# Summing part of the second attention's weights on GpSimd in the first and the last batch element

## The chip, the cores and the metric

The kernel runs on one core of a Trainium2 chip. The metric is the device time in microseconds (us). The kernel before was run 7 times: median 3838.09 us, lowest 3835.74, highest 3838.99.

A core has five engines that run their own instruction streams in order and wait for each other through semaphores: TensorE (PE in the profile; its weight loads are listed as PEld), VectorE (DVE), ScalarE (ACT), GpSimd (POOL) and SyncE (SP, which here only issues DMAs).

## The reference, cut to what matters

The input holds 16 batch elements of 256 channels x 1024 positions, all in f32. Each element passes an attention of 4 heads of 64 (called a), a group norm, an attention of 8 heads of 32 (called b), a second group norm, and a two-layer network of 1024 hidden channels. Only attention b is touched by the change:

```python
attn = jnp.einsum('bhnd,bhmd->bhnm', q, k) * scale + phys_bias
attn = jax.nn.softmax(attn, axis=-1)
out = jnp.einsum('bhnm,bhmd->bhnd', attn, v)
```

The softmax divides each exponential by the sum of the exponentials over all 1024 keys. The kernel takes no maximum out first; it computes the exponentials e, multiplies them by v unnormalised, sums them up over the keys beside that, and divides at the end.

## The kernel before, in words

`first_pass` goes through the elements b = 0 to 15. Work of neighbouring elements is interleaved by hand: while `attention_b` of element b runs, `run` puts pieces of other work ("fill") between its steps: first the rest of its own query, key and value products, then the output products of the network of element b-1 and the query, key and value products of element b+1. Element 0 has no element before it, and its fill is only its own products. The last element has its own products and four pieces of the network of element 14; the other four of those pieces come after the attention. So in both of these elements some steps of `attention_b` stand bare, with nothing put between them.

`attention_b` (line 398 on) works through four items. An item is one block of 512 queries for one group of 4 heads (128 channels). An item is done in four units, at kb = 0, 2, 4 and 6; a unit covers two blocks of 128 keys. For each unit:

- `scores` (L422) makes 16 matmuls on PE, into all eight banks of PSUM: for the first key block two single banks (b0, b1) and one tile of two banks, for the second key block two tiles of two banks. ACT turns them into four SBUF tiles e of 128x1024 with five exponentials (L437). A matmul in f32 shows as two records in the trace, two passes.
- `add(..., 0)` adds the first two e tiles (first key block, head pairs 0 and 1) to the item's two sums `es` on DVE (L452). At kb = 0 there is nothing to add to yet, and `add(..., 1)` makes the sums from two pairs of tiles.
- `weigh` (L461) of the unit before runs on PE: 8 matmuls of e with v into bank b0. Its result is copied to `res` by ACT for kb = 0 (L475) and added to it by DVE for the others (L477). Only then can the next unit's scores use b0.
- `add(..., 1)` adds the other two e tiles to the sums, and is held in program order on DVE (`keep_in_program_order` puts an instruction behind the last one written for its engine).

The e tiles have 8 buffers, so a tile is written over two units later, after PE and the adding engine have read it.

When an item's last `weigh` has been issued, `normalise` follows one step later, that is at the end of the next item's first unit: 4 matmuls `den` (L485), one per head, against the ones-like weights `eones`, into bank b1. They add the sums over the 128 partitions; each writes 32 of the 128 PSUM partitions. `den_copy` (L282) copies the bank out on ACT, and the next unit's scores need b1 again. `denominators` then sends the rows to a compact tile by DMA on SP's queue, takes the reciprocal on DVE (L267), keeps two running checks on GpSimd (`dsum`, `isum`, L269 and L270), sends the reciprocals out and back in by DMA, and `scale` multiplies `res` by them on DVE (L500). After the second head group, `project` follows (`j`, PE).

The order on each engine is what a scheduler makes of the written order: an instruction goes early where its inputs are free, and the pinned ones stay.

## Time and profile before

The profiled execution took 3838.63 us, with a span of 3836.9 us from the first to the last instruction on the core; 1.7 us lie around it.

| | busy us | share of the span |
|---|---|---|
| PE | 3782.7 | 99% |
| PEld | 1509.3 | 39% |
| DVE | 2213.9 | 58% |
| ACT | 2033.8 | 53% |
| POOL | 84.7 | 2% |

The TensorE clock was granted at 0.999 of full speed. A busy share is a mean over stages of different kinds, and the end of a matmul is modelled, so PE at 99% doesn't mean that PE sets the pace everywhere. Where a group's line ends with "idle before, releaser", it tells how long the engine stood still before these instructions and what ended that. In a timeline, a row gives the start of a run of equal instructions, its length, engine, line, operation, tiles and, in brackets, the idle time just before it and what ended it. Times in it are counted from the start of the span.

### The profile page before, as it was taken

Reading aid. Unit: us, or ns where it says so; the run is one execution under the profiler, and the core shown is the slowest. Engines: PE = TensorE matmul, PEld = TensorE weight load, DVE = VectorE, ACT = ScalarE, POOL = GpSimd, SP = SyncE. Lnnn points to the kernel's source line nnn. Section 1 sums busy time; section 2 is a strip of 40 time slices with the busy share of each in tenths; the row PEclk is TensorE's granted clock in tenths of the full one; section 3 lists DMA queues with packets and bytes.
Section 4 is the critical chain, followed back from the end, with each engine's and each line's share of the span. In section 5 each row is a group of like instructions: output and inputs, shape, how many; then the busy total and the mean of one; then the engine's idle time right before and its main releaser. Section 6 shows DMA issues by size and latency. Waiting matters only on the chain.

```text
span 3836.9 us, 87391 instructions
## 1 busy us (share of the span) xinstructions
PE 3782.7 (99%) x38637; PEld 1509.3 (39%) x38637; DVE 2213.9 (58%) x2761; ACT 2033.8 (53%) x2625; POOL 84.7 (2%) x252
## 2 busy tenths in 40 slices
PE   8999999999999999999999999999999999999999
PEld 3334343333433334333343333433333333333435
DVE  4574646646466464665656556565564655646572
ACT  4555546555465554645546455454555545555461
POOL 1000000000000000000000000000000000000000
PEclk9999999999999999999999999999999999999999
DMA  2000000000000000000000001000000100000000
GB/s 83 10 16 12 30 12 16 27 12 30 12 16 27 12 30 12 19 29 7 30 12 22 26 10 32 7 33 15 13 30 7 32 15 13 29 7 25 12 13 23
DMA packets 62450, 78.58 MB, mean 20 GB/s; under 512 B 35344, under 2 KB 36880, under 8 KB 62064
## 3 DMA queue, kind: packets, MB, share of 16 engines
q1 hardware_dynamic: 57728, 68.72, 5.9%
q8 instruction: 304, 4.98, 0.5%
q10 hardware_dynamic: 3712, 3.80, 0.3%
q14 instruction: 82, 0.67, 0.1%
q0 software_dynamic: 624, 0.41, 0.0%
HBM read 54.54 MB, written 17.56 MB: 19 GB/s over the span
## 4 chain that ended last, share of the span: by engine, by line
PE 90%; DVE 5%; issue 2%; ACT 2%; DMA 0%; POOL 0%; ACTq 0%; SPq 0%; POOLq 0%; DVEq 0%
PE s_b L422 12%; PE m L709 12%; PE acc_b L461 12%; PE m L246 11%; PE s_a L303 10%; PE acc_a L324 9%; PE qk_b L246 6%; PE qk_a L246 6%; PE v_b L246 3%; PE j L246 3%; PE v_a L246 3%; DVE es_a L336 2%; PE o L246 2%; PE den_b L485 1%; ACT e_a L311 1%
## 5 line engine op out<-in xcount | busy, mean ns | idle before, releaser
L437 ACT ACTIVATE e_b<-s_b 128x1024 f32<-128x1024 f32 (+1 forms) x1280 | 982.7, 864 | 469.3 <-PE s_b L422 469.3
L452 DVE TENSOR_TENSOR es_b<-es_b,e_b 128x1024 f32<-128x1024 f32 x768 | 900.0, 1220 | 361.2 <-ACT e_b L437 361.2
L311 ACT ACTIVATE e_a<-s_a 128x1024 f32<-128x1024 f32 x512 | 521.4, 1025 | 450.1 <-PE s_a L303 438.2
L303 PE MATMUL s_a<-q,k 64*64 64x512 f32 x4096 | 562.2, 593 | 2.3 <-DVE x L533 2.3
L324 PE MATMUL acc_a<-e_a,v 64*64 64x512 f32 x4096 | 555.2, 589 | 0.0
L422 PE MATMUL s_b<-q,k 32*64 32x512 f32 x8192 | 536.3, 601 | 5.8 <-DVE res_b L477 4.9
L336 DVE TENSOR_TENSOR es_a<-es_a,e_a 128x1024 f32<-128x1024 f32 x384 | 469.0, 1221 | 111.5 <-ACT e_a L311 106.7
L461 PE MATMUL acc_b<-e_b,v 128*32 128x512 f32 x4096 | 492.1, 598 | 0.0
L709 PE MATMUL m<-gn_h,w 128*128 128x512 f32 x1024 | 459.9, 601 | 6.0 <-DVE mean_g L569 3.8
L246 PE MATMUL m<-g,w 128*32 128x256 f32 (+1 forms) x7616 | 464.0, 379 | 0.0
L246 PEld LDWEIGHTS m<-g,w 128*32 128x32 f32 (+1 forms) x7616 | 277.7, 112 | 215.8 <-issue 41.5
L717 ACT ACTIVATE g<-m,m1b 128x512 f32<-128x512 f32 x256 | 174.3, 687 | 341.9 <-PE m L709 341.7
L422 PEld LDWEIGHTS s_b<-q,k 32*64 32x64 f32 x8192 | 173.8, 130 | 293.9 <-issue 155.7
L324 PEld LDWEIGHTS acc_a<-e_a,v 64*64 64x64 f32 x4096 | 183.5, 133 | 260.6 <-issue 224.6
L709 PEld LDWEIGHTS m<-gn_h,w 128*128 128x128 f32 x1024 | 189.0, 190 | 244.4 <-issue 227.3
L303 PEld LDWEIGHTS s_a<-q,k 64*64 64x64 f32 x4096 | 167.5, 133 | 280.3 <-issue 199.1
L461 PEld LDWEIGHTS acc_b<-e_b,v 128*32 128x32 f32 x4096 | 108.5, 109 | 351.6 <-ACT e_b L437 194.7
L246 PE MATMUL qk_a<-x,wp 128*32 128x512 f32 (+1 forms) x1856 | 234.5, 594 | 9.4 <-DMA wp<-in_L_conv_w_proj_dram 6.5
L477 DVE TENSOR_TENSOR res_b<-res_b,acc_b 128x512 f32<-128x512 f32 x192 | 131.0, 682 | 190.9 <-PE acc_b L461 190.9
L246 PE MATMUL qk_b<-gn_g,wq 128*32 128x512 f32 (+1 forms) x1280 | 234.1, 592 | 0.0
L452 DVE TENSOR_TENSOR es_b<-e_b,e_b 128x1024 f32<-128x1024 f32 x128 | 150.7, 1219 | 52.4 <-ACT e_b L437 52.4
L639 DVE TENSOR_TENSOR v<-v_b,eones 128x512 f32<-128x512 f32 x64 | 43.8, 685 | 227.8 <-PE v_b L246 227.8
(112 smaller groups left out, 2068.7 us busy)
## 6 DMA issues: line engine op xcount, KB each, us to landing
x<-in_x_dram SPq DMA_DIRECT2D x32, 512.0 KB
rd_a<-row_a SPq DMA_DIRECT2D x64, 256.0 KB
rd_b<-row_b SPq DMA_DIRECT2D x256, 64.0 KB
out_dram<-x SPq DMA_DIRECT2D x64, 256.0 KB
w<-in_L_conv_mlp_w_dram ACTq DMA_DIRECT2D x2, 1024.0 KB
sp_b<-d_b SPq DMA_DIRECT2D x64, 8.0 KB
row_b<-inv_b SPq DMA_DIRECT2D x64, 8.0 KB
wq<-in_L_conv_qkv_w_dram ACTq DMA_DIRECT2D x1, 768.0 KB
```

Of the source, the lines that this page charges most:

```text
L246: nc.tensor.matmul(o[sl], w[:, sl], r, **flags)
L303: nc.tensor.matmul(s[h : h + HALF, g, :], kT[g * D : (g + 1) * D, c, kb * P + h : kb * P + h + HALF], qT[g * D : (g + 1) * D, c, t * TB : ...
L311: nc.scalar.activation(e, s, AF.Exp, scale=float(D) ** -0.5)
L324: nc.tensor.matmul(accs[i][h][g * D : (g + 1) * D, :], v[h * HALF : (h + 1) * HALF, kb, c * 2 + g], e[h * HALF : (h + 1) * HALF, g, :], st ...
L336: nc.vector.tensor_add(sums[i], held[i] if kb == 1 else sums[i], e)
L422: nc.tensor.matmul(outs[g][h : h + HALF, :], kT[g * D : (g + 1) * D, c, k0 : k0 + HALF], qT[g * D : (g + 1) * D, c, t * TB : (t + 1) * TB] ...
L437: nc.scalar.activation(to, s, AF.Exp, scale=float(D) ** -0.5)
L452: ins = nc.vector.tensor_add(d, es[n] if kb == 0 else d, es[2 * block + n])
L461: nc.tensor.matmul(acc[g * D : (g + 1) * D, :], v[:, kb + m, c * G + g], es[2 * m + g // 2][:, g % 2, :], start=(m == 0), stop=(m == 1),)
L477: nc.vector.tensor_add(r, r, acc)
L709: nc.tensor.matmul(ps, k["w1"][:, cc, hc * P : (hc + 1) * P], hn[0][:, cc, t * TB : (t + 1) * TB], start=(cc == 0), stop=(cc == CC - 1),)
L717: nc.scalar.activation(g, ps, AF.Gelu, bias=k["m1b"][:, hc : hc + 1])
```

## The change

In elements 0 and 15 alone, and only for units with kb = 2, 4 and 6, one of the two additions of `add(..., 1)`, that of head pair 1, is taken off DVE. GpSimd sums these tiles instead, into two tiles of 128x512 of their own (`apart`): it copies the two halves at kb = 2 and adds the two halves at kb = 4 and at kb = 6. In element 0 the tiles come from the buffers of the hidden layer (tag "g", 16 buffers); in element 15 they lie in a tile over the query buffer of attention a, which is free by then. `normalise` then has, for the heads of pair 1, two matmuls per head in place of one: the second adds the apart sums to the same PSUM rows.

```diff
+        helped, apart = b in (0, B - 1), {}
+        if b == B - 1:
+            spare = act.tile([P, CC, S], F32, tag="q0", name=f"spare_{key}")
...
             for n in range(G // 2):
                 d = sums[i][n]
+                if helped and block and n and kb:
+                    if kb == 2:
+                        apart[i] = [
+                            spare[:, i % 2, j * TB : (j + 1) * TB] if b else
+                            work.tile(
+                                [P, TB], F32, tag="g", name=f"ges_{key}_{i}_{j}", bufs=16
+                            )
+                            for j in range(2)
+                        ]
+                    for j, a in enumerate(apart[i]):
+                        e = es[2 * block + n][:, j, :]
+                        if kb == 2:
+                            nc.gpsimd.tensor_copy(a, e)
+                        else:
+                            nc.gpsimd.tensor_add(a, a, e)
+                    continue
                 ins = nc.vector.tensor_add(d, es[n] if kb == 0 else d, es[2 * block + n])
...
             for g in range(G):
-                nc.tensor.matmul(
-                    den[g * D : (g + 1) * D, :],
-                    k["eones"][:, c * G + g],
-                    sums[i][g // 2][:, g % 2, :],
-                    start=True,
-                    stop=True,
-                )
+                parts = [sums[i][g // 2][:, g % 2, :]]
+                if helped and g // 2:
+                    parts.append(apart[i][g % 2])
+                for m, part in enumerate(parts):
+                    nc.tensor.matmul(
+                        den[g * D : (g + 1) * D, :],
+                        k["eones"][:, c * G + g],
+                        part,
+                        start=(m == 0),
+                        stop=(m == len(parts) - 1),
+                    )
```

## The prediction

> **What bounds the kernel now.** I read the page's engine shares and its chain first, then windows over the two elements that change, then a timeline of one item in the bare stretch, then the POOL rows. On the page, PE leads with 99% and the chain that ended last is PE's:

> ```profile
> PE 90%; DVE 5%; issue 2%; ACT 2%; DMA 0%; POOL 0%; ACTq 0%; SPq 0%; POOLq 0%; DVEq 0%
> ```

> In elements 1 to 14 nothing is changed, so only the stage matters. Windows (length, then busy time of PE, PEld, DVE, ACT, POOL) show attention b of element 0 from its second item on, and the last element with fill and bare:

> ```profile
> 163.54:185.01 21.47, 19.94 (x204) 5.07 (x201) 18.74 (x20) 16.40 (x23) 1.28 (x2) 1.00 0.06 14
> 185.01:206.49 21.48, 19.95 (x205) 5.08 (x201) 18.75 (x20) 16.41 (x23) 1.29 (x2) 1.00 0.05 15
> ...
> 3683.41:3710.10 26.69, 26.69 (x396) 11.04 (x393) 18.44 (x22) 15.50 (x21) 0.22 (x1) 1.00 0.10 32
> ```

> A bare item takes 21.5 us and DVE is busy for 18.7 of them: near full, not full. With fill (last row) PE has no gap at all. So I went through a bare item row by row, in the timeline:

> ```profile
> 170.50 3.83 ACT L437 ACTIVATE e_b<-s_b 128x512 f32<-128x512 f32 x5 [1.17 <-PE s_b L422]
> ...
> 171.62 2.36 DVE L452 TENSOR_TENSOR es_b<-es_b,e_b 128x1024 f32<-128x1024 f32 x2 [0.66 <-ACT e_b L437]
> ...
> 173.90 0.68 DVE L477 TENSOR_TENSOR res_b<-res_b,acc_b 128x512 f32<-128x512 f32 x1
> 174.50 2.35 DVE L452 TENSOR_TENSOR es_b<-es_b,e_b 128x1024 f32<-128x1024 f32 x2
> ...
> 174.64 1.97 PE L422 MATMUL s_b<-q,k 32*64 32x512 f32 x30 [0.43 <-DVE res_b L477]
> ...
> 176.77 0.69 DVE L500 TENSOR_TENSOR res_b<-res_b,rd_b 128x512 f32<-128x512 f32 x1
> 177.37 2.35 DVE L452 TENSOR_TENSOR es_b<-es_b,e_b 128x1024 f32<-128x1024 f32 x2
> ...
> 179.64 0.68 DVE L477 TENSOR_TENSOR res_b<-res_b,acc_b 128x512 f32<-128x512 f32 x1
> 180.38 1.97 PE L422 MATMUL s_b<-q,k 32*64 32x512 f32 x30 [0.92 <-DVE res_b L477]
> ...
> 184.02 1.04 PE L485 MATMUL den_b<-es_b,eones 128*32 128x512 f32 x8
> 185.18 0.63 ACT L282 COPY d_b<-den_b 128x512 f32<-128x512 f32 x1
> ```

> The unit starts (first of the scores) lie at 163.54, 169.38, 174.64, 180.38 and 185.01, so the four steps of an item are 5.84, 5.26, 5.74 and 4.63. What ends each: the first, ACT (exponentials, then the copy of `res`, for which PE waits). The second, a latency: scores, exponentials (start 170.50), the two block-0 adds from 171.62 on, `res`, scores; DVE stood idle 0.66 ahead of it, so fewer adds don't shorten it. The third is the same loop, but DVE comes late: it still has the block-1 adds (174.50) and the multiplication (176.77) in hand. The fourth is PE: scores, `acc`, `den`, and the copy of `den` on ACT, which the next scores on bank b1 need.

> **What the change removes.** 24 adds of 128x1024 (two elements, four items, three units), 24 x 1.22 = 29 us of DVE. On the path lies only the third step, and there only what it has above the loop of the second: 5.74 - 5.26 = 0.48. It stands bare at three places (174.64 to 180.38, 196.11 to 201.85, 3721.20 to 3726.94). With fill, PE sets the step; at the fourth item's end too (`j` at 221.23 and 3746.32 follow `acc` without a gap). The most to be gained is 3 x 0.48 = 1.4 us.

> **What it adds on PE.** Eight times, two more matmuls, four more records. Eight records now start within 1.0 us in two rounds of four, 0.43 apart (the four heads sit on different columns of the array, and run side by side). The extra ones sit on the columns of heads 2 and 3, so these two need four rounds: 2 x 0.43 = 0.86 more. That the two heads' chains run side by side I take from the scores at 169.38: after one of the 16 matmuls went ahead alone, the first round holds eight records where the written order has a repeat of a position at the eighth, so a later matmul on a free position starts early:

> ```profile
> 169.38 0.71 PE L422 MATMUL s_b<-q,k 32*64 32x512 f32 x8 [0.18 <-ACT res_b L475]
> ```

> [...]

> Is it hidden? With fill, and where attention a or the network follows (`den` at 226.38, 3678.99, 3751.47), PE is full: 0.86 each. In the bare stretch the first scores (b0) wait for `res` until 184.95 anyhow, but b1 waits for the copy of `den`, which starts 0.1 after `den` ends, and the second exponential waits for b1 (0.25 idle). So all but some 0.06 passes on: 0.8. The sum is 8 x 0.8 = 6.4 us.

> **What it adds on GpSimd.** 16 copies and 32 adds of 128x512, for which there is no row. A memset on POOL takes 0.127 us for 128x16 and 0.223 for 128x128: 0.86 ns an element. The add of `dsum`, 128x16, takes 0.22. Lower end for the big add: 0.22 + 496 x 0.86 ns = 0.65 us (one pass). Upper end: two reads and a write in three passes, 1.5 us. I take two passes, 1.07, since two inputs must be read; a copy is 0.13 + 0.43 = 0.55.

> [...]

> GpSimd has the time: 5.4 us of a 21.5 us item. What counts is whom it stops. POOL's `dsum` takes 0.22 as a rule, but where it meets an es add it waits for its end:

> ```profile
> 166.38 1.06 POOL L269 TENSOR_TENSOR dsum<-dsum,sp_b 128x16 f32<-128x16 f32 x1 [44.41 <-DMA sp_b<-d_b]
> ...
> 166.14 4.66 DVE L452 TENSOR_TENSOR es_b<-es_b,e_b 128x1024 f32<-128x1024 f32 x4 [0.39 <-ACT e_b L437]
> ```

> The first of these four adds ends at 167.36, `dsum` at 167.44, between the first and the second. It goes the other way too: where POOL began 0.03 us ahead, the es add took 1.27 instead of 1.22:

> ```profile
> 467.17 0.22 POOL L270 TENSOR_TENSOR isum<-isum,inv_b 128x16 f32<-128x16 f32 x1
> ...
> 467.20 1.27 DVE L336 TENSOR_TENSOR es_a<-e_a,e_a 128x1024 f32<-128x1024 f32 x1 [0.17 <-ACT e_a L311]
> ```

> So a POOL add and a DVE add from two SBUF tiles exclude each other, and take turns. A short POOL read costs DVE 0.05; a read of 1.07 would cost about 1.

> Now the third step. The exponentials of the unit end at 170.50 + 3.83 = 174.33, and POOL's two adds are ready some 0.14 later (the delay from DVE's reciprocal to `isum`), just as DVE starts its remaining block-1 add at 174.50. Taking turns: DVE add 1.15 (pitch), POOL 1.07, DVE multiplication 0.6, POOL 1.07, two block-0 adds 2.3. `res` then starts at 174.50 + 6.19 = 180.69 instead of 179.64: 1.05 late, though an add has gone. [...] I take +1.0, three times: 3.0 us.

> At kb = 2 the copies meet a DVE that has 0.66 to spare and one add less; with fill the step has about 2 us of slack between `res` and the next scores. Nothing. At the end of the fourth item POOL's last add comes late for `den`: 222.69 ready, after the block-0 add at 223.64, POOL to 224.71, DVE's add to 225.85, POOL to 226.9 against `den` at 226.38 now. About +0.5 in both elements (0 to 1.2): 1.0 us. The tiles are free two units later than POOL needs them, SP's queue gets no new DMA, and behind POOL's new adds stand only `dsum` and `isum`, which nobody but the end check waits for.

> **The sum.** 6.4 + 3.0 + 1.0 = +10.4 us on 3838.63 of the profiled execution, 3849.0. That execution lies 0.5 above the median of the runs; I say 3849.

> **Rivals.**
> - *POOL stops nobody* (not slower): long reads share with DVE instead of excluding it. Place: the third step at its three bare places. Price: 6.4 - 1.4 = +5.0, 3843.6, within 0.2%. It decides as soon as the blocked time per POOL add falls below about 0.55. For it: the trace shows exclusion only with reads of 16 elements. Against: eight of eight met adds end 0.08 after the DVE add.
> [...]
> [...]
> - *`den` hidden*: the extra rounds run beside the next scores on heads 0 and 1's columns and b1 isn't waited for. Only 4.0, or 3842.6; with POOL harmless as well, the full gain, 3837.2.

> **How the numbers follow.** The forecast has 0.42, long adds 0.20, POOL harmless 0.20, strict order 0.08, `den` hidden 0.04, both hidden 0.06. What a measurement of this kernel can tell from no change is about 0.2%, 7.7 us: above 3845.8 is slower, below 3830.4 faster. Slower: 0.20 + 0.08 and nearly nine tenths of the forecast, 0.64. Faster: no case reaches it; 0.03 for a scheduler that orders things differently. Same: the rest, 0.33. The range from 3840 to 3858 leaves out only the full gain and what is worse than the long adds.

> **What would show it.** After: `den_b` with 12 records in four rounds, about 1.7 us long; POOL rows of 128x512, and their length; es adds on DVE of over 2 us in the bare units, or none; the third step at about 6.7 us or at 5.26; the fourth at about 5.4. I am wrong if long POOL reads don't hold DVE, if a POOL add is far from 1.07, or if the scheduler changes DVE's order.

## The result and the profile after

The changed kernel took 3847.09 us (median of 15 runs, 3845.59 to 3849.21), the kernel before beside it 3837.12 us (median of 35). That is 10.0 us slower; the ratio is 1.0026, with a 95% interval of 1.0019 to 1.0033. The profiled execution took 3847.57 us, with a span of 3845.8 us, 8.9 us more than the span before.

The page hardly shows it. These are the chain's shares and two groups of the changed kernel (a group's columns: busy us, mean ns of one, idle us before it and what ended that):

```profile
PE 90%; DVE 5%; ACT 2%; issue 2%; DMA 0%; POOL 0%; SPq 0%; ACTq 0%; POOLq 0%; DVEq 0%
...
L475 DVE TENSOR_TENSOR es_b<-es_b,e_b 128x1024 f32<-128x1024 f32 x744 | 880.6, 1231 | 375.4 <-ACT e_b L437 375.4
...
L422 PE MATMUL s_b<-q,k 32*64 32x512 f32 x8192 | 537.3, 603 | 8.9 <-DVE res_b L500 8.0
```

The same two groups before:

```profile
L452 DVE TENSOR_TENSOR es_b<-es_b,e_b 128x1024 f32<-128x1024 f32 x768 | 900.0, 1220 | 361.2 <-ACT e_b L437 361.2
...
L422 PE MATMUL s_b<-q,k 32*64 32x512 f32 x8192 | 536.3, 601 | 5.8 <-DVE res_b L477 4.9
```

DVE has lost its 24 adds, and yet PE's scores stood idle for DVE's `res` for 8.0 us, where the kernel before has 4.9. The mean of DVE's remaining adds went up, from 1220 to 1231 ns. These two lines fit what was expected of GpSimd, that it stands in DVE's way.

The time by steps needs the unit starts (first of the scores) of the two elements. An item has four units; the steps of the 16 units, in us, with the last one counted to the next matmul group:

| | items 1, 2, 3, 4 before | after |
|---|---|---|
| element 0 | 6.76 7.20 7.20 5.54; 4.63 5.85 5.25 5.74; 4.63 5.85 5.25 5.74; 4.63 5.85 5.25 9.76 | 6.75 7.20 7.20 5.47; 5.50 5.77 5.25 6.76; 5.49 5.77 5.25 6.77; **7.00** 5.77 5.25 10.64 |
| sum | 95.15 | 101.86 |
| element 15 | 6.76 7.20 7.20 5.54; 8.07 7.21 7.21 7.63; 4.64 5.85 5.25 5.74; 4.63 5.85 5.25 9.76 | 6.76 7.20 7.20 5.47; 8.95 7.21 7.21 7.59; 5.50 5.77 5.25 6.78; 5.49 5.77 5.25 10.64 |
| sum | 103.79 | 108.04 |

The prediction's "fourth step" (scores, `acc`, `den`, copy of `den`) opens a row's item here, because `den` of an item lies in the first unit of the next: 4.63 before, 5.50 after. Its "third step" is the item's last number: 5.74 before, 6.77 after. Between the two elements, from the end of element 0 to the first scores of element 15, nothing moved: 3421.30 us before, 3421.28 after.

So element 0 costs 6.7 us more and element 15 4.25 more, 10.96 in all. It comes from four sources: `den` eight times 0.86 to 0.88, together 6.9; the bare third step three times 1.03, 3.1; one step of 7.00 where its two fellows take 5.49, 1.5; and small gains of 0.04 to 0.08 in eight steps, 0.6 less. The span grew by less than 10.96, because in this execution the program's first scores came 2.1 us earlier. That is no gain of the change: over the profiles of this study the first scores came at any time from 129.5 to 132.5 us. In the kernel before they came at 132.20, and the granted clock was 0.50 from 16.42 to 19.82; in the changed kernel they came at 130.09, with a clock of 1.00 from 5 to 25.

The second item of element 0 in the changed kernel, from its second unit on (timeline of all engines; rows of weight loads and of SP are left out):

```profile
172.50 0.68 DVE L500 TENSOR_TENSOR res_b<-res_b,acc_b 128x512 f32<-128x512 f32 x1
173.08 4.04 POOL L473 TENSOR_TENSOR ges_b<-ges_b,e_b 128x512 f32<-128x512 f32 x2 [3.26 <-ACT e_b L437]
173.10 1.22 DVE L475 TENSOR_TENSOR es_b<-es_b,e_b 128x1024 f32<-128x1024 f32 x1
173.24 1.97 PE L422 MATMUL s_b<-q,k 32*64 32x512 f32 x30 [0.43 <-DVE res_b L500]
...
174.56 1.43 DVE L527 TENSOR_TENSOR res_b<-res_b,rd_b 128x512 f32<-128x512 f32 x1 [0.24 <-DMA rd_b<-row_b]
...
175.13 1.92 PE L484 MATMUL acc_b<-e_b,v 128*32 128x512 f32 x16
175.91 3.44 DVE L475 TENSOR_TENSOR es_b<-es_b,e_b 128x1024 f32<-128x1024 f32 x2
...
176.99 1.07 PE L422 MATMUL s_b<-q,k 32*64 32x512 f32 x2
...
179.27 0.68 DVE L500 TENSOR_TENSOR res_b<-res_b,acc_b 128x512 f32<-128x512 f32 x1
...
180.00 1.97 PE L422 MATMUL s_b<-q,k 32*64 32x512 f32 x30 [1.94 <-DVE res_b L500]
...
183.64 1.06 PE L512 MATMUL den_b<-es_b,eones 128*32 128x512 f32 x8
...
184.51 1.05 PE L512 MATMUL den_b<-ges_b,eones 128*32 128x512 f32 x4
...
185.63 0.58 ACT L282 COPY d_b<-den_b 128x512 f32<-128x512 f32 x1 [0.67 <-PE den_b L512]
```

Two things are to be seen. PE's scores at 180.00 stand idle for 1.94 us instead of 0.92, because `res` starts at 179.27. And `den` has a second row at 184.51, so its copy starts 1.99 us after its first record instead of 1.16.

The turns show one by one in the third item, where the timelines of DVE and of POOL in narrow windows keep the instructions apart:

```profile
196.38 1.22 DVE L475 TENSOR_TENSOR es_b<-es_b,e_b 128x1024 f32<-128x1024 f32 x1
...
197.51 1.76 DVE L527 TENSOR_TENSOR res_b<-res_b,rd_b 128x512 f32<-128x512 f32 x1
...
199.20 2.30 DVE L475 TENSOR_TENSOR es_b<-es_b,e_b 128x1024 f32<-128x1024 f32 x1
...
201.42 1.21 DVE L475 TENSOR_TENSOR es_b<-es_b,e_b 128x1024 f32<-128x1024 f32 x1
...
202.56 0.67 DVE L500 TENSOR_TENSOR res_b<-res_b,acc_b 128x512 f32<-128x512 f32 x1
```

```profile
196.36 2.36 POOL L473 TENSOR_TENSOR ges_b<-ges_b,e_b 128x512 f32<-128x512 f32 x1 [3.26 <-ACT e_b L437]
...
198.69 1.73 POOL L473 TENSOR_TENSOR ges_b<-ges_b,e_b 128x512 f32<-128x512 f32 x1
```

Waiting for the other engine is not shown as idle time but as a longer instruction. POOL's first add is 2.36 long, of which it waits out DVE's add (to 197.60). DVE's multiplication is 1.76 instead of 0.68: held by 1.08. DVE's first block-0 add is 2.30 instead of 1.22: held by 1.08 again.

### The profile page after: what moved, and what is told of

Read it like the earlier page. It is cut to its first block, busy times and chain, and to the rows that moved or that the text cites. A ratio compares the mean times of both kernels' runs of the same rounds, so it can differ in the third digit from the quotient of the medians.

```text
span 3845.8 us, 87438 instructions
## 1 busy us (share of the span) xinstructions
PE 3790.2 (99%) x38669; PEld 1514.9 (39%) x38669; DVE 2200.2 (57%) x2737; ACT 2033.4 (53%) x2625; POOL 159.0 (4%) x300
## 4 chain that ended last, share of the span: by engine, by line
PE 90%; DVE 5%; ACT 2%; issue 2%; DMA 0%; POOL 0%; SPq 0%; ACTq 0%; POOLq 0%; DVEq 0%
PE s_b L422 12%; PE m L736 12%; PE acc_b L484 12%; PE m L246 11%; PE s_a L303 10%; PE acc_a L324 9%; PE qk_b L246 6%; PE qk_a L246 6%; PE v_b L246 3%; PE j L246 3%; PE v_a L246 3%; DVE es_a L336 2%; PE den_b L512 2%; PE o L246 2%; ACT e_b L437 1%
## 5 line engine op out<-in xcount | busy, mean ns | idle before, releaser
L437 ACT ACTIVATE e_b<-s_b 128x1024 f32<-128x1024 f32 (+1 forms) x1280 | 982.5, 865 | 473.5 <-PE s_b L422 473.5
L475 DVE TENSOR_TENSOR es_b<-es_b,e_b 128x1024 f32<-128x1024 f32 x744 | 880.6, 1231 | 375.4 <-ACT e_b L437 375.4
L311 ACT ACTIVATE e_a<-s_a 128x1024 f32<-128x1024 f32 x512 | 520.7, 1024 | 450.6 <-PE s_a L303 438.0
L422 PE MATMUL s_b<-q,k 32*64 32x512 f32 x8192 | 537.3, 603 | 8.9 <-DVE res_b L500 8.0
L336 DVE TENSOR_TENSOR es_a<-es_a,e_a 128x1024 f32<-128x1024 f32 x384 | 468.9, 1221 | 111.6 <-ACT e_a L311 106.4
L422 PEld LDWEIGHTS s_b<-q,k 32*64 32x64 f32 x8192 | 174.8, 130 | 296.2 <-issue 161.6
L500 DVE TENSOR_TENSOR res_b<-res_b,acc_b 128x512 f32<-128x512 f32 x192 | 131.1, 683 | 196.6 <-PE acc_b L484 196.6
L475 DVE TENSOR_TENSOR es_b<-e_b,e_b 128x1024 f32<-128x1024 f32 x128 | 150.8, 1219 | 52.4 <-ACT e_b L437 52.4
```

What stands on the lines that cost most here:

```text
L311: nc.scalar.activation(e, s, AF.Exp, scale=float(D) ** -0.5)
L336: nc.vector.tensor_add(sums[i], held[i] if kb == 1 else sums[i], e)
L422: nc.tensor.matmul(outs[g][h : h + HALF, :], kT[g * D : (g + 1) * D, c, k0 : k0 + HALF], qT[g * D : (g + 1) * D, c, t * TB : (t + 1) * TB] ...
L437: nc.scalar.activation(to, s, AF.Exp, scale=float(D) ** -0.5)
L475: ins = nc.vector.tensor_add(d, es[n] if kb == 0 else d, es[2 * block + n])
L500: nc.vector.tensor_add(r, r, acc)
```

## The experiments

All times are medians beside the kernel before on the same chip; where a ratio stands, 9 to 11 runs are behind it, otherwise one. "Body" is the change of the two elements' step sums against those of before, from the profile of the run.

### The two parts of the change, each alone

**Only the longer `den`.** On the changed kernel, DVE does all the adds again, and GpSimd only fills its tiles with zeros for the second matmuls to read:

```diff
-                    for j, a in enumerate(apart[i]):
-                        e = es[2 * block + n][:, j, :]
-                        if kb == 2:
-                            nc.gpsimd.tensor_copy(a, e)
-                        else:
-                            nc.gpsimd.tensor_add(a, a, e)
-                    continue
+                        for a in apart[i]:
+                            nc.gpsimd.memset(a, 0.0)
```

> All adds back on DVE; GpSimd only writes zeros once per item (kb = 2), and the two extra den matmuls per item read these zeros. Theory (eight longer den stages, and GpSimd's reads in the way of DVE at three places): the den part alone, 8 x 0.86 = 6.9 us above before; the steps of a bare item 5.8, 5.26, 5.74, 5.5 us; no gap on PE above 1 us. Rival (all of the loss comes from GpSimd holding DVE): no change against before. Rival (den hidden in the bare stretch, only the three full places pay): 2.6 us above before.

Measured: 3844.76 against 3837.40, +7.4, ratio 1.0019 (1.0010 to 1.0028). Body +3.23 in element 0 and +3.36 in element 15. Every step with `den` is 0.86 to 0.88 longer, the third step is still 5.74 and its gap 0.92:

```profile
181.00 1.97 PE L422 MATMUL s_b<-q,k 32*64 32x512 f32 x30 [0.92 <-DVE res_b L495]
...
184.64 1.06 PE L507 MATMUL den_b<-es_b,eones 128*32 128x512 f32 x8
185.51 1.05 PE L507 MATMUL den_b<-ges_b,eones 128*32 128x512 f32 x4
```

From the start of `den` to the end of its last record it is 1.92 us, 0.87 of it added. About seven of the ten microseconds are this.

**Only GpSimd's adds.** On the changed kernel, the second matmuls of `den` are dropped:

```diff
-                if helped and g // 2:
-                    parts.append(apart[i][g % 2])
```

> As the changed kernel, but den is left with its four matmuls, so the part that GpSimd sums is missing from the denominators. Theory: 3 x 1.02 = 3.1 us above before from the third step, less 0.2, and 1.5 more in an execution where the TensorE clock falls to half behind a gap; 3 to 4.5 us above before, third step 6.76, fourth step 4.63. Rival (den makes up all of the loss): at or 1.4 us below before.

Measured: 3843.52 against 3837.40, +6.1, ratio 1.0017 (1.0008 to 1.0026). That is more than expected. The steps tell why: the third step is 6.77, as in the changed kernel, so GpSimd's price is there, three times 1.03. But the step behind it is 4.64 once, and 6.29 and 6.31 the other two times in element 0. There the granted TensorE clock was halved. PE's rows at the first of these places:

```profile
179.06 3.60 PE L422 MATMUL s_b<-q,k 32*64 32x512 f32 x30 [1.95 <-DVE res_b L500]
...
184.35 1.03 PE L510 MATMUL den_b<-es_b,eones 128*32 128x512 f32 x8
```

Thirty score records take 3.60 us instead of 1.97. A window over this place (length; busy us of PE, PEld, DVE, ACT, POOL; granted clock; DMA share; GB/s) gives the clock:

```profile
179.00:183.00 4.00, 3.94 (x34) 1.06 (x38) 1.62 (x2) 2.08 (x4) 2.74 (x2) 0.57 0.01 2
```

So there is a third term that the prediction doesn't have: some 1.7 us on the step behind each halved clock. Without these two longer steps the body would be +2.7.

**GpSimd writes zeros, DVE keeps its relief.** On the changed kernel, the copies and adds become zero fills:

```diff
-                        if kb == 2:
-                            nc.gpsimd.tensor_copy(a, e)
-                        else:
-                            nc.gpsimd.tensor_add(a, a, e)
+                        nc.gpsimd.memset(a, 0.0)
```

> As the changed kernel, but GpSimd fills its tiles with zeros in place of copying and adding, so it reads nothing; the part that it would sum is missing from the denominators. Theory (a GpSimd read of two inputs and a DVE add of two SBUF inputs exclude each other): no DVE add above 1.3 us, third step 5.26, no gap of 1.9 us on PE and no halved clock; 6.9 - 3 x 0.48 - 0.2 = 5.3 us above before. Rival (the loss in the third step comes from GpSimd's writes or its mere presence): third step stays at 6.7, as the changed kernel, 10 us above before.

Measured: 3842.94 against 3837.40, +5.5, ratio 1.0013 (1.0004 to 1.0022). The third step is 5.25 in all three places. Rows of the second item (all engines) and GpSimd's group:

```profile
175.90 0.69 DVE L524 TENSOR_TENSOR res_b<-res_b,rd_b 128x512 f32<-128x512 f32 x1
...
177.12 2.36 DVE L472 TENSOR_TENSOR es_b<-es_b,e_b 128x1024 f32<-128x1024 f32 x2 [0.53 <-ACT e_b L437]
...
180.13 1.97 PE L422 MATMUL s_b<-q,k 32*64 32x512 f32 x30 [0.43 <-DVE res_b L497]
```

```profile
L470 POOL MEMSET ges_b<- x24: 527/527/543, 17.0 to 28.1; 128x512 f32 x24
```

The last row limits what this run says. The fills have no input, so the scheduler put those of element 0 at the program's start, from 17.0 to 28.1 us; in the bare third steps there is no fill in either element. There the run is DVE's relief with GpSimd absent. It confirms that a DVE with one add less would reach the loop's 5.25 (the multiplication takes 0.69, and DVE then stands idle for 0.53), so what took the gain away in the changed kernel is GpSimd's work in that step. Fills in that very step were not tried, but in element 15 some run beside DVE's adds: six in a row from 3713.17 to 3716.03, each of 0.52 or 0.53 us, while the adds that start at 3713.21 and 3715.62 take 1.22 and 1.23. So in these rows a GpSimd instruction that only writes neither holds such an add nor waits for it.

**GpSimd's add at kb = 4 given back to DVE.** Only the add that meets the third step is moved back:

```diff
-                if helped and block and n and kb:
+                if helped and block and n and kb in (2, 6):
```

> As the changed kernel, but the add at kb = 4 is back on DVE; GpSimd copies at kb = 2 and adds at kb = 6. Theory (only GpSimd's adds at kb = 4 stand in the loop, since those of kb = 6 become ready as the second block-0 add starts): third step 5.7 as before the change, fourth 5.5, 6.9 - 0.2 = 6.7 us above before. Rival (each GpSimd add costs its own time on DVE, wherever it lies): two thirds of the 3.1 us stay, and the third step is 6.4.

Measured: 3845.24 against 3837.40, +7.8, ratio 1.0019 (1.0010 to 1.0028); body +3.23 and +3.33, the same as with the longer `den` alone. The third step's rows:

```profile
176.85 2.35 DVE L475 TENSOR_TENSOR es_b<-es_b,e_b 128x1024 f32<-128x1024 f32 x2
...
179.15 3.49 POOL L473 TENSOR_TENSOR ges_b<-ges_b,e_b 128x512 f32<-128x512 f32 x2 [8.45 <-ACT e_b L437]
...
179.85 1.97 PE L422 MATMUL s_b<-q,k 32*64 32x512 f32 x30 [0.92 <-DVE res_b L500]
```

The adds at kb = 6 still run on GpSimd (179.15) and the copies at kb = 2 too, and neither moves a step. GpSimd's whole price is in the one add at kb = 4, in the three bare third steps.

### The halved clock

**A longer gap with no GpSimd work.** On the kernel before, DVE gets two useless adds of 128x512 in the third step:

```diff
+                if b in (0, B - 1) and block and n and kb == 4:
+                    for j in range(2):
+                        a = spare[:, i % 2, j * TB : (j + 1) * TB] if b else work.tile(
+                            [P, TB], F32, tag="g", name=f"ges_{key}_{i}_{j}", bufs=16
+                        )
+                        e = es[2 * block + n][:, j, :]
+                        tc.keep_in_program_order(nc.vector.tensor_add(a, e, e))
```

> The kernel before, with nothing on GpSimd and den as it was; at kb = 4 in elements 0 and 15 DVE makes two more adds of 128x512, whose result nobody reads, so PE's gap in the third step grows from 0.92 to about 2.1 us. Theory (the halved TensorE clock behind the gap in the changed kernel comes from the length of the gap and from where it lies): 3 x 1.2 = 3.6 us above before, and in element 0 or 15 at one or two of the three gaps a clock of 0.5 for 3.4 us, 1.5 us each: 3.6 to 7. Rival (GpSimd's activity halves the clock): no halved clock within the two elements, 3.6 us.

Measured: 3848.27 against 3837.47, +10.8, ratio 1.0029 (1.0019 to 1.0039). More than expected, for a reason beside the question: the two adds also lengthen the third step with fill (5.54 to 6.75 in the first item of both elements, 7.63 to 8.84 in the second of element 15) and the two ends (9.76 to 10.19), which I had left out. For the question itself, PE's rows and the window over the place:

```profile
203.13 3.56 PE L422 MATMUL s_b<-q,k 32*64 32x512 f32 x30 [2.13 <-DVE res_b L487]
```

```profile
203.00:206.40 3.40, 3.27 (x30) 0.88 (x30) 2.35 (x3) 1.25 (x3) 0.00 (x0) 0.50 0.02 5
```

POOL's column is 0.00, and the clock is 0.50. The step is 6.22 instead of 4.63. The clock fell behind a gap of PE that DVE alone had made; it took no work of GpSimd's. It happened in one of this run's three gaps of 2.13.

**The changed kernel once more.** No edit; a second profile of it, to see whether the halved clock comes back at the same place.

> The changed kernel once more, for a second profile: the steps as in the first, 5.5, 5.77, 5.25, 6.77. Theory (whether the clock halves behind a gap depends on where the gap falls): with another start of attention b a halved clock at none, one or two of the three gaps, not always the same one. Rival (it belongs to the third item of element 0): again there.

One run: 3849.89 us. All steps are as in the first profile, except that the clock is halved twice, in element 0 and in element 15 (the step in element 15 is 7.14 there, 5.49 in the first profile):

```profile
202.50:205.90 3.40, 3.16 (x30) 0.88 (x30) 1.80 (x2) 1.14 (x3) 2.92 (x2) 0.51 0.00 0
3735.30:3738.70 3.40, 3.40 (x26) 0.59 (x16) 0.36 (x1) 3.40 (x5) 1.49 (x1) 0.51 0.00 0
```

For comparison, the first profile of the changed kernel (a full item, and the place at the third item's end):

```profile
180.00:203.28 23.28, 20.72 (x204) 5.42 (x204) 17.98 (x17) 16.51 (x22) 10.88 (x9) 0.99 0.06 14
203.28:206.69 3.41, 3.41 (x31) 0.90 (x31) 1.56 (x1) 1.39 (x3) 2.68 (x2) 0.54 0.00 0
```

The first profile has the step of 7.00 there, and the second one is hit at that place again (7.05). The rival, that the halved clock belongs to the third item of element 0, falls all the same: in this profile element 15 is hit too, and in the run with only GpSimd's adds and in the one below the second item of element 0. Which of the three gaps is hit changes from one execution to the next.

### The order of the matmuls in `den`

On the changed kernel, all first matmuls are written ahead of all second ones, so that even a strict order has nothing to hold up:

```diff
-            for g in range(G):
-                parts = [sums[i][g // 2][:, g % 2, :]]
-                if helped and g // 2:
-                    parts.append(apart[i][g % 2])
-                for m, part in enumerate(parts):
+            for m in range(2 if helped else 1):
+                for g in range(G):
+                    pair = helped and g // 2
+                    if m and not pair:
+                        continue
...
-                        part,
+                        apart[i][g % 2] if m else sums[i][g // 2][:, g % 2, :],
```

> The changed kernel, but with the four first den matmuls written ahead of the two second ones. Theory (a matmul on free columns starts ahead of an earlier one on busy columns): no change, den in four rounds as now, fourth step 5.5. Rival (strict order, the four rounds of the changed kernel being due to something else): the fourth step changes by 0.4 us or more.

One run: 3848.92 us; the step with `den` is 5.47 against 5.50 (and once 6.81, a halved clock).

```profile
161.50 1.04 PE L512 MATMUL den_b<-es_b,eones 128*32 128x512 f32 x8
162.37 1.03 PE L512 MATMUL den_b<-ges_b,eones 128*32 128x512 f32 x4
```

The written order is worth 0.03 us. The changed kernel's `den` already ran nearly as if it had been written this way: eight records of `es`, then four of `ges`, although the code issues head 2's second matmul ahead of head 3's first. It isn't that the scheduler had made the two programs alike: in all eight `den` of the changed kernel head 3's record of the second round starts 0.030 us behind head 2's, in all eight of this run 0.007. But no view shows the order in which PE was given the matmuls; that head 3 overtook on PE follows from the order of the code.

### What does help in these steps

The third step has 0.48 us above its loop, and the loop itself has two adds on DVE ahead of `res`. Both can be had by order alone, without GpSimd.

**The multiplication later.** On the kernel before, the multiplication `res_b<-res_b,rd_b` is written one step later for the first two items:

```diff
-                ((3, 5) if b + 1 < B else (1, 1)) if last else (1, 1),
+                ((3, 5) if b + 1 < B else (1, 1)) if last
+                else (1, 2) if b in (0, B - 1) and i < 2 else (1, 1),
```

> The kernel before, with nothing on GpSimd and den as it was; only the multiplication by the reciprocals (L500) of the first two items comes one unit later in elements 0 and 15, into DVE's idle time at the item's end. Theory (in the third step DVE has 0.48 too much in hand, and no more is to be had by taking work off DVE): third step 5.26, 3 x 0.48 = 1.4 us below before, not to be told from no change by the clock alone. Rival (DVE's load as such sets the bare items): no change of the steps, since DVE does as much as before.

Measured: 3836.43 against 3837.47, ratio 0.9996 (0.9987 to 1.0005). Too small to be told from no change by the times, but the steps have it: 5.25 in place of 5.74 in all three bare third steps, body -0.98 and -0.59. (In element 15 the third step with fill falls too, from 7.63 to 7.21, but there PE has the fill to do, and the next step rises by as much, from 4.64 to 5.06.) The 0.48 that the prediction took for all that DVE's relief could bring is real, and is to be had for nothing.

**`res` first.** On the kernel before, the second block-0 add is put behind `weigh`, so that `res` comes one add earlier:

```diff
-        def add(i, kb, es, block):
+        def add(i, kb, es, block, pairs=(0, 1), pin=False):
...
-            for n in range(G // 2):
+            for n in pairs:
...
-                if block:
+                if block or pin:
...
-            add(*now, 0)
+            split = b in (0, B - 1)
+            add(*now, 0, (0,) if split else (0, 1))
...
+            if split:
+                add(*now, 0, (1,), True)
```

> The kernel before, but in elements 0 and 15 the second block-0 add stands behind the addition of acc to res on DVE, so that the next scores wait for one add less. Theory (the second step is a latency through scores, exponentials, block-0 adds and res): the step falls from 5.26 to about 4.6 at five places (scores, 1.9; acc, 1.9; res, 0.7), the third stays near 5.7, since DVE is then full: about 3.3 us below before (2 to 4). Rival (DVE's load sets both steps): no change.

Measured: 3838.21 against 3837.47, ratio 1.0002 (0.9993 to 1.0011): the expectation failed. The second step fell further than expected, from 5.25 to 3.75, so the block-0 adds stand in the latency loop, as the prediction had it. But DVE is nearly full in a bare item (18.7 of 21.5 us), and an add put off is not an add saved: the third step rose to 6.62, the fourth item's end from 9.76 to 11.01 and 11.16, and the third step with fill from 5.54 to 6.06. Of 7.5 us gained in five second steps, 0.4 was left.

**Both.** The two edits together.

> The edits of the later multiplication and of res ahead of the second block-0 add together. Theory: second step 4.6, third about 5.1, 5 x 0.67 + 3 x 0.6 = 5.1 us below before. Rival: as before.

Measured: 3835.15 against 3837.47, ratio 0.9993 (0.9984 to 1.0002); body -2.2 and -0.2, less than half of what was expected. The third step is 6.02 with the multiplication out of the way; the first items' step with fill (6.06) and the ends (11.01) keep their losses.

**Both, but `res` first only where the item is bare.** On the kernel with both edits:

```diff
-            split = b in (0, B - 1)
+            split = u[0] >= {0: 1, B - 1: 2}.get(b, len(items))
```

> The kernel before with the later multiplication, and with res ahead of the second block-0 add only where the steps are bare: the last three items of element 0, the last two of element 15. Theory, from the steps measured with both edits everywhere: bare items with second and third step of 3.75 + 6.02 in place of 5.25 + 5.74 (1.22 less, three times), the fourth item's end 0.25 less (twice), the steps with fill as before: 4.3 us below before. Rival (the steps gained come back at the end of the element): no change.

Measured: 3834.71 against 3838.23, -3.5, ratio 0.9991 (0.9982 to 1.0000). Body -2.70 and -1.57, together the 4.3 expected. The rows of a bare item:

```profile
170.95 1.23 DVE L454 TENSOR_TENSOR es_b<-es_b,e_b 128x1024 f32<-128x1024 f32 x1 [0.67 <-ACT e_b L437]
...
172.60 0.69 DVE L479 TENSOR_TENSOR res_b<-res_b,acc_b 128x512 f32<-128x512 f32 x1 [0.43 <-PE acc_b L463]
173.20 4.62 DVE L454 TENSOR_TENSOR es_b<-es_b,e_b 128x1024 f32<-128x1024 f32 x4
...
177.75 0.68 DVE L479 TENSOR_TENSOR res_b<-res_b,acc_b 128x512 f32<-128x512 f32 x1
...
178.48 1.97 PE L422 MATMUL s_b<-q,k 32*64 32x512 f32 x30 [0.32 <-DVE res_b L479]
...
181.75 0.68 DVE L503 TENSOR_TENSOR res_b<-res_b,rd_b 128x512 f32<-128x512 f32 x1
```

After one add, `res` waits 0.43 for `acc` and no longer for the second add; the put-off adds follow at 173.20 in a run of four, and PE's gap at the third step is 0.32 instead of 0.92. This is the fastest version of the study, 3.5 us below the kernel before; its interval just reaches 1.0000.

## Why the prediction was right, step by step

**What bounds the stage: right.** Beside the named steps none moved by more than 0.08, but for those behind a halved clock. The latency loop, DVE's lateness of 0.48 in the third step and the place of `den` on PE's path were each moved by an experiment of their own (the second step to 3.75, the third to 5.25, the fourth to 5.50).

**`den`: right, a little small.** The term was eight times 0.8; it is 0.86 to 0.88. The slack of 0.06 that the prediction took off isn't there: the whole of the two rounds passes on. The first step's -0.08, which I hadn't foreseen, came in the five bare items of the run with the longer `den` alone, too (5.77 four times, 5.80 once). With it the net of that run, 3.23 + 3.36 = 6.6, is nearer to the predicted 6.4 than the parts are.

**No strict order in `den`: right, with PE's overtaking argued from the order of the code.** The case "strict order", with 0.08 among the prediction's chances, has the matmuls of `den` start in the order of the code, head 3's first behind head 2's second; by my estimate that would be six rounds. Three things in the runs speak against it. `den` runs in four rounds (starts at 183.64, 184.07, 184.51 and 184.94 in the second item); the order written out takes 5.47 against 5.50; and with fill, records of the next group start between the records of `den`, two every 0.22 us, and four every 0.22 from 3685.23 on, 0.43 behind the start of `den`'s last. That fits columns that `den` leaves free (PE's rows in element 15; where the scheduler put `m` in PE's order isn't shown):

```profile
3683.50 1.06 PE L512 MATMUL den_b<-es_b,eones 128*32 128x512 f32 x8
3684.36 0.39 PE L246 MATMUL m<-g,w 128*32 128x256 f32 x2
3684.37 0.62 PE L512 MATMUL den_b<-spare_b,eones 128*32 128x512 f32 x2
3684.57 0.60 PE L246 MATMUL m<-g,w 128*32 128x256 f32 x4
3684.80 0.62 PE L512 MATMUL den_b<-spare_b,eones 128*32 128x512 f32 x2
```

By these rows "in order", as the first section has it of the engines, goes too far for the starts of PE's matmuls.

The rival "`den` hidden" gets its chance here, and doesn't use it: although `m` begins between the records of `den`, the step with fill grew by the full 0.88 (8.07 to 8.95).

**GpSimd's turns in the third step: right to 0.02 us, on a wrong duration.** The prediction had `res` start 6.19 us after DVE's remaining block-1 add. It is 202.56 - 196.38 = 6.18 in the third item and 179.27 - 173.10 = 6.17 in the second. The step grew by 1.03, with +1.0 predicted. The rows of GpSimd's two forms (minimum, median and maximum in ns, then first and last start) give the duration:

```profile
L473 POOL TENSOR_TENSOR ges_b<-ges_b,e_b x16: 1277/2206/2367, 149.1 to 228.5; 128x512 f32<-128x512 f32 x16
L471 POOL COPY ges_b<-e_b x8: 605/612/1183, 141.9 to 217.3; 128x512 f32<-128x512 f32 x8
```

An add that nobody holds takes 1.28 us, not the assumed 1.07. By the prediction's turns the second block-0 add starts at 174.50 + 1.15 + 0.6 + 1.15 = 177.40 plus two POOL adds, and the next unit's tile is ready at 179.73 (ACT's exponentials run from 175.76 for 3.83 in the kernel before, and 0.14 comes on top). So by that estimate adds above 1.17 let a third POOL add in ahead of it: the case "long adds", with 0.20 among the chances. The add was longer than that, and the case didn't come, because of those 1.28 us GpSimd holds DVE for only 1.08: the multiplication went from 0.68 to 1.76, the block-0 add from 1.22 to 2.30. My 1.07 was a wrong duration that happened to be the right length of the hold: luck. And it was close: the next unit's GpSimd add starts at 201.61, 0.19 after DVE's second block-0 add (201.42), and so comes too late to get in ahead of it. By these rows, a hold longer by some 0.1 for each of the two adds would have let it come in first.

**"POOL stops nobody": fell.** The third step would have been 5.25, as in the run without GpSimd work there; it is 6.77. That the add at kb = 4 is the whole of it, the run that gave this add back to DVE shows.

**The ends of the fourth item: wrong, +0.5 predicted, nothing measured.** The end grew by 0.88, and by the same 0.88 with the longer `den` alone. GpSimd's last add does come about as late as I worked out: it ends at 230.79, 9.49 after the unit's start at 221.30, with 9.3 predicted. But I compared it with the start of `den`. The first eight records need only `es`; the four that need GpSimd's tiles come 0.87 later, at 230.96, and by then the add is done, 0.17 ahead. In one step of the prediction I had put the rounds that read GpSimd's tiles behind the others, and in the other step I let the whole of `den` wait for GpSimd.

**The halved clock: not in the prediction.** About 1.5 us each time, behind one of three bare third steps in the first profile and behind two of three in the second. It is what fills the place of the ends' 1.0 in the sum: 6.9 + 3.1 - 0.6 = 9.4 from the steps, and 1.5 or 3.2 from the clock, 11.0 and 12.7 in the two profiles; the medians, over runs in which the first scores can come up to 3 us apart, have 10.0. That the total of +10.4 came so close is thus partly luck: a term that was not there and a term that was missed are of like size.

## What to carry to other kernels

Here work given to GpSimd was no relief for DVE where GpSimd read SBUF while DVE had an instruction with two SBUF operands to do: two adds of 1.28 us on GpSimd held DVE for 1.08 each, to spare it a single add of 1.22. (`res`, with one operand in PSUM, took 0.68 at 179.27, beside a GpSimd add, as it does elsewhere. GpSimd's copies, with one SBUF operand, waited for such a DVE add as well: 1.18 where they met one, 0.61 otherwise.) Look for the step in which the two meet, and move the work to a step where nobody waits for DVE (the copies and the adds at kb = 6 cost nothing). And ask first what ends the step: reordering two instructions on DVE alone, in the bare items alone, brought 4.3 us by the steps and 3.5 by the medians, while the change could have gained 1.4 at the most, and paid 6.9 on PE for splitting a sum in two.

## What the runs showed of the hardware that was not expected

The grid tells the 7 gaps from the 8. Ahead of the gap PE has only one early score matmul on a 32x64 part of the array (176.99 to 178.06 in the second item's rows). For each window of the grid one can add up the time in which PE is idle or runs one such record and nothing else. In the seven windows at whose end the clock fell, it is 2.15 to 2.82 us; in none of the other 14161 windows that began at full clock, from 25 to 3750 us in the thirteen profiles, is it more than 1.98 (the ends of matmuls are modelled, so the border between is rough). So in these profiles it is how much of the gap and of the record ahead of it falls into one window that sorts them. In the first profile the window from 199.56 to 202.97, ahead of the halved clock, has 2.48. The gap of element 15, from 3732.15 to 3734.11, is cut at 3732.35 there, neither window has more than 1.76, and the clock stays at 1.00; in the second it lies, from 3732.15 to 3734.10, whole in a window that ends at 3735.34, which has 2.18, and there the clock falls. Idle time alone doesn't sort the windows: the clock fell after 1.31 us of it (after 1.64 in the first profile, to 202.97) and held after 1.75 (there as well, from 3732.35).

**DVE is held for less than GpSimd's instruction lasts.** DVE's instructions with two SBUF operands and GpSimd's adds exclude each other, and take turns instruction by instruction (2.36 for a GpSimd add that met a DVE add, 1.76 for the multiplication behind it); but DVE went on 1.08 us into GpSimd's 1.28. Whether GpSimd lets go before its end, or spends the rest without reading, no run here shows.

**Steps with no direct cause.** The first step of the bare items became 0.08 shorter with the longer `den` (5.85 to 5.77). The copy of `den` on ACT is shorter there, 0.58 instead of 0.63, but why the step gains is not settled.
